# A conv-attention and mixture-of-experts layer on one core: where the expert gates' transfers are issued inside a step

## The chip, the core and the metric

The kernel runs on 1 core of one Trainium2 chip. The metric is the device time of one execution in microseconds (us), lower being better. Five engines with their own instruction streams work side by side: TensorE (PE in the profile; its weight loads are PEld), VectorE (DVE), ScalarE (ACT), GpSimd (POOL) and SyncE (SP). SP computes nothing here; it issues nearly all transfers between DRAM and the on-chip memory, one after the other, and waits at each until what the transfer depends on is done.

## The reference

The input `x` is 2 x 128 x 256 x 256 in float32. The layer does two things to it.

```python
x = x + attention(ln_over_channels(x))        # 8x8 windows, keys from 12x12, 4 heads of 32,
                                              # a fixed mask, relative positions, out projection
t = tokens(x)                                 # 131072 tokens of 128 channels
p = softmax(ln(t) @ router_w + router_b)      # 8 experts
g, e = top_2(p);  g = g / sum(g)
t = t + sum over the two: g * (ln(t) @ expert_w[e] + expert_b[e])
```

Of the mask only keys at every second row and column are left, so the image falls into four independent planes (row parity by column parity), and a window has 4 x 4 queries and 6 x 6 keys in a plane.

## The kernel before

**Strips, planes, steps.** The image is worked in 64 strips of 8 rows (32 for each of 2 images). Each strip has 4 planes, so there are 256 planes, and the main loop runs over `n`, one plane a step, with 7 more steps at the end to drain what follows. A step does attention for plane `n` (`scores`, `attend`, `out_project`), the projections for plane `n + 1` (`project`), the norms of one row pair (512 tokens) of a finished strip and of one row pair of a coming strip (`norms`), and, for older row pairs, the routing (`route`, `spread`) and the experts (class `Experts`). The order on each engine is written out by hand: all five engines run what the loop emits, in that order (`manual_schedule`).

**The experts.** All 8 experts are computed for all tokens: the input, less its mean and times expert e's gate, is multiplied with expert e's weights, and the 8 products are summed in PSUM (`product`, L714: 2 matmul instructions each, 16 a step). A gate is one number for each token. `spread` transposes the gates (`gT`, L651) and writes them to a small DRAM buffer `gd` (L659). From there `fetch(e)` reads one expert's 512 gates into a tile `gb` and copies them to all 128 partitions on the way (L689, 256 KB written); `fetch_means` does so for the means (`sb`, L694) and `fetch_rstd` for the scale of the coming row pair (`rb`, L665). Ahead of each gate's transfer stands a tiny write into the tile (L686 a ScalarE copy, L688 a VectorE memset). It paces the transfer: SP can't issue it before that engine has come to this place in its order.

**Three objects at a time.** `new` is the row pair whose gates are fetched in this step; a step later it is `nxt`, and its multiplications run: `means` (L699, `xs`: input plus `sb`), then `times(e)` (L705, `xe` = `xs` * `gb`) on VectorE for experts 0, 1, 2, 3, 4, 6 and on GpSimd for 5 and 7. Then it is `ex`: products 0 to 3 end that step and products 4, 6, 7, 5 stand in the middle of the next, followed by `end` (L720: the sum is added to the image, and the row pair is stored, L750).

**Gates before.** `gb` has 8 buffers, one a gate. Gates 0, 1, 2 are paced by memsets among VectorE's multiplications, 3 and 6 by memsets later in its order, 4 by a ScalarE copy after the norms. Gates 5 and 7 are fetched in the next step, through `nxt`: 5 behind ScalarE's exponential of the routing (L618), 7 behind its copy of the values (L358). SP's order in a step is:

```text
gd, gd, vrows (1 or 2), rb, sb, vwin, vwin, gate 0, 1, 2, xt (load), gate 3, out (store),
gate 4, gate 6 | next step: gate 5, gate 7
```

**Values.** `send_values` writes the value rows of plane `n + 1` to DRAM (`vrows`, L369); `take_values` reads them back as windows (`vwin`, L381), in two transfers of 240 KB, one for each half of the partitions. The first waits for the `vrows` writes to land.

**GpSimd.** Each step it runs `behind(6)` (L709, a one-element copy that waits for VectorE's `times(6)`), `times(5)`, `ln1` (L276, which needs `rb`), in every fourth step `halo` (L250), and `times(7)`.

**TensorE's code.** Its instructions are laid out in blocks of `BLOCK` = 256. At the start of each step of 6 or more, `addr_align` (L823) places the step so that `FIRST_LIMIT` = 95 instructions lie ahead of the first block boundary; the next boundaries come after 351 and 607. A weight load and a matmul are one instruction each. In a step 32 + 128 pairs (L474, L491), then `pu` 2, `pv` 8, `pk` 2 and `pq` 2 pairs come first, so the boundary after 351 falls just behind the first pair of the expert products (L714), and the one after 95 inside L491.

**DMA counters.** The built program gives the transfers eight completion counters in turn; an issue waits until the transfer eight before it has landed.

Of the kernel before, what the change touches and what calls it, by code (L numbers as in the profile page):

```python
# [11 lines left out]
F32 = mybir.dt.float32  # L12
# [5 lines left out]
P = 128  # L18
# [33 lines left out]
def kernel(  # L52
# [16 lines left out]
    nc = tc.nc  # L69
# [8 lines left out]
    NT = CH // P  # L78
# [7 lines left out]
    gates = ctx.enter_context(tc.tile_pool(name="gates", bufs=2))  # L86
# [18 lines left out]
    def load_x(i, k, paced=False):  # L105

        if i >= len(strips):
            return
        b, s = strips[i]
        if k == 0:  # L110
            xt[i] = xpool.tile([P, R, W], F32, tag="xt", name=f"xt{i}")
        r = s * R + 2 * k
        if paced:
            nc.scalar.copy(xt[i][:, 2 * k, 0:1], onesm[:, 0:1])
        nc.sync.dma_start(xt[i][:, 2 * k : 2 * k + 2, :], x[b, :, r : r + 2, :])
# [248 lines left out]
    def send_values(n, sent):  # L364

        i, pl = divmod(n, 4)
        for part, vr in sent:
            for k, at, m in runs(i, part):
                nc.sync.dma_start(  # L369
                    vrows[pl][1 : PC + 1, at : at + m, :],  # L370
                    vr[:, k - part[0] : k - part[0] + m],
                )

    def take_values(n):

        for half in range(2):
            src = vrows[n % 4][half * HP * 8 : half * HP * 8 + KC].rearrange("c r d -> (c r) d")
            src = src.unsqueeze(1)
            dims = [list(d) for d in src.ap]
            dims[1] = [8 * KR * P, HP]  # L380
            nc.sync.dma_start(  # L381
                vwin[n % 2][half * SLOT : half * SLOT + NK],
                bass.AP(src.tensor, src.offset, dims),
            )
# [77 lines left out]
    def scores(n, state):  # L462


        qs, kk, au = state["qs"], state["kk"], state["au"]
        turn = place(n // 4, 0) // 2
        att = ps_att.tile([P, 4, 512], F32, tag="att", name=f"att{n}")
        sc = att[:, :, 0:HQ]
        for w in range(2):
            for half in range(2):  # L470
                rows = slice(half * SLOT, (half + 1) * SLOT)
                for h in range(HEADS):
                    hp = slice(h * DH, (h + 1) * DH)
                    nc.tensor.matmul(  # L474
                        sc[rows, h].rearrange("p (t w z) -> p t w z", w=2, z=16)[:, :, w],
                        lhsT=keys[hp, turn, w],
                        rhs=au[hp, half * NP + w : (half + 1) * NP : 2].rearrange(
                            "p t a s -> p t (a s)"
                        ),
                        start=(w == 0),  # L480
                        stop=False,
                    )
        for t in range(HP):
            if t == HP // 2:
                yield
            for half in range(2):
                rows = slice(half * SLOT, (half + 1) * SLOT)
                m0 = 2 * (half * HP + t)
                for h in range(HEADS):
                    hp = slice(h * DH, (h + 1) * DH)  # L490
                    nc.tensor.matmul(  # L491
                        sc[rows, h, 32 * t : 32 * t + 32],
                        lhsT=kk[hp, half * HP + t, :],
                        rhs=qs[hp, m0 : m0 + 2].rearrange("p m a s -> p (m a s)"),
                        start=False,
                        stop=(t == HP - 1),
                    )
        pT = work.tile([P, HEADS, HQ], F32, tag="pT", name=f"pT{n}", bufs=1)
        nc.scalar.activation(pT, att[:, :, 0:HQ], AF.Exp)  # L499
        state.update(att=att, pT=pT)  # L500
        yield
# [166 lines left out]
    def to_all(gd, j):  # L668

        return gd[j * NT : (j + 1) * NT].rearrange("r k -> (r k)").partition_broadcast(P)  # L670

    class Experts:
# [7 lines left out]
        def fetch(self, e, eng):  # L680


            nm = "_".join(str(v) for v in (*self.at, e))
            self.gb[e] = gates.tile([P, NT * P], F32, tag="gb", name=f"gb{nm}", bufs=8)
            if eng is nc.scalar:
                eng.copy(self.gb[e][:, 0:1], onesm[:, 0:1])  # L686
            else:
                eng.memset(self.gb[e][:, 0:1], 0.0)  # L688
            nc.sync.dma_start(self.gb[e], to_all(self.gd, e))  # L689
# [55 lines left out]
    to_store = []  # L745

    def store(i, k):
        b, s = strips[i]
        r = s * R + 2 * k
        nc.sync.dma_start(out[b, :, r : r + 2, :], xt[i][:, 2 * k : 2 * k + 2, :])  # L750
        if k == R // 2 - 1:
            xt.pop(i)
# [4 lines left out]
    n_planes = 4 * len(strips)  # L757
# [45 lines left out]
    gated, ex, nxt = None, NoExperts(), NoExperts()  # L803
    last = ctile([P, 1], "last")
    pool, dve = nc.gpsimd, nc.vector

    ET = mybir.EngineType
    with tc.manual_schedule(engines={ET.PE, ET.DVE, ET.Activation, ET.Pool, ET.SP}):
        for n in range(n_planes + 7):
            i, pl = divmod(n, 4)  # L810
            score, attn, outp, ahead, norm, rout = none, none, none, none, none, none
            if n < n_planes:
                score = scores(n, states[n])
                attn = attend(n, states[n])
                outp = out_project(n, states[n])
            if n + 1 < n_planes:
                states[n + 1] = {}
                ahead = project(n + 1, states[n + 1])

            if 6 <= n < n_planes:
                nc.tensor.addr_align(BLOCK, offset=BLOCK - FIRST_LIMIT)  # L823


            next(score, None)
            new, row = NoExperts(), None
            if gated and gated[0]:
                rout = route(*gated[0], *gated[2])
            next(rout, None)  # L830
            nxt.fetch(5, nc.scalar)
            for _ in rout:
                pass
            next(score, None)
            next(ahead, None)
            nxt.fetch(7, nc.scalar)
            if gated:
                f, c, made = gated
                gd = spread(f, c, made[0], f"_{n}")
                new = Experts(*f, gd) if f else new  # L840
            if n + 1 < n_planes:
                send_values(n + 1, states[n + 1]["sent"])
            if gated and c:
                row = (*c, fetch_rstd(gd, f"_{n}"))
            next(ahead, None)
            if n + 1 < n_planes:
                states[n + 1]["shift"]()
            next(ahead, None)
            next(ahead, None)
            for e in (4, 6, 7, 5):  # L850
                ex.product(e)


            f = (i - 1, pl) if 0 < i <= len(strips) else None
            c = row_at(n)
            if f or c:
                norm = norms(f, c, f"_{n}")
            next(norm, None)
            next(attn, None)
            nxt.means()  # L860
            new.fetch_means()
            if n + 1 < n_planes:
                take_values(n + 1)
            for e in (0, 1, 2, 3):
                nxt.times(e, dve)
            new.fetch(0, dve)
            for e in (4, 6):
                nxt.times(e, dve)
            new.fetch(1, dve)
            ex.end()  # L870
            new.fetch(2, dve)
            next(attn, None)
            next(attn, None)


            ex = nxt
            next(norm, None)
            load_x((n + 9) // 4, (n + 9) % 4, paced=True)
            new.fetch(3, dve)
            while to_store:  # L880
                store(*to_store.pop())
            next(ahead, None)
            ex.product(0)
            made = next(norm, None)
            ex.product(1)
            ex.product(2)
            new.fetch(4, nc.scalar)
            nxt.behind(6)
            nxt.times(5, pool)
            if row:  # L890
                ln1(*row, pool)
            if pl == 3 and i + 2 < len(strips):
                halo(i + 2)
            nxt.times(7, pool)
            if n + 2 < n_planes:
                borders(n + 2)
            next(outp, None)
            ex.product(3)
            next(outp, None)
            new.fetch(6, dve)  # L900
            gated, nxt = (f, c, made) if made else None, new
            states.pop(n, None)

# [58 lines left out]
```

## Time and profile before

| | |
|---|---|
| time, median of 3 runs (lowest to highest) | 4413.72 us (4412.22 to 4419.66) |
| the profiled execution: its time, its span | 4415.92 us, 4414.1 us |
| granted TensorE clock, mean | 0.992 |
| PEld busy | 2453.1 us (56%) |
| VectorE busy | 3844.2 us (87%) |
| ScalarE, GpSimd busy | 1455.9 us (33%), 1092.5 us (25%) |
| HBM read and written | 863.78 and 143.75 MB, 228 GB/s over the span |

The page of the profile gives the busy time of each engine, the costliest groups of instructions (line, engine, operation, what is written and read, number, busy time and mean, and the idle time ahead of them with what ended it), the transfers by kind with the median time from issue to landing, and the DMA queues. The view of waits lists who waited for whom: total, number of times, longest. The timeline lists instructions in order of time: start in us, duration in us, engine, line, operation, tile, and in brackets the idle time ahead of it. "issue" there means that the profile shows nothing waited for. The view of windows gives each engine's busy time in a stretch and, last, the mean busy share of the DMA engines and the rate in GB/s.

### The profile page before, as it was taken

What the parts mean: (1) busy time and instruction counts of PE and PEld (TensorE: products, weight loads), DVE (VectorE), ACT (ScalarE), POOL (GpSimd) and SP (SyncE); (2) the same over time, 40 slices, a digit from 0 to 9 for tenths busy, and PEclk for the clock granted to TensorE, in tenths of its full rate; (3) what the DMA queues carried; (4) which work ended last, traced back from release to release, by engine and by line L of the source; (5) the groups of instructions that cost most, each with busy time, mean ns of one, the idle gap of its engine ahead of it and who ended that gap; (6) DMA issues with size and microseconds to landing.
All of it is one profiled execution on the core that took longest, in us unless ns stands there. A gap on an engine that the chain in (4) does not pass through costs nothing. (4 is left out here: it accounts for less than half of the span.)

```text
span 4414.1 us, 224656 instructions
## 1 busy us (share of the span) xinstructions
PE 4254.2 (96%) x94273; PEld 2453.1 (56%) x94273; DVE 3844.2 (87%) x11850; ACT 1455.9 (33%) x3774; POOL 1092.5 (25%) x1126
## 2 busy tenths in 40 slices
PE   7899999999999999999999999999999999999987
PEld 4555555555555555555555555555555555555553
DVE  5788889888898988898888889988888888888877
ACT  3333333333333333333333333333333333333321
POOL 1122222222222222222222222222222222222211
PEclk9999999999999999999999999999999999999998
DMA  4677777777787777777878777777778777777865
GB/s 121 201 246 229 244 232 241 246 234 233 233 242 232 242 238 235 244 234 243 243 233 243 231 242 232 243 239 239 242 229 244 238 236 233 232 232 239 243 195 183
DMA packets 824580, 1022.19 MB, mean 232 GB/s; under 512 B 137634, under 2 KB 409634, under 8 KB 823594
## 3 DMA queue, kind: packets, MB, share of 16 engines
q1 hardware_dynamic: 822864, 1007.52, 74.6%
q8 instruction: 769, 12.60, 1.2%
q14 instruction: 217, 1.78, 0.1%
q10 hardware_dynamic: 730, 0.29, 0.0%
HBM read 863.78 MB, written 143.75 MB: 228 GB/s over the span
## 5 line engine op out<-in xcount | busy, mean ns | idle before, releaser
L714 PE MATMUL acc<-xe,ew 128*128 128x512 f32 x4096 | 1935.8, 602 | 66.7 <-issue 44.9
L714 PEld LDWEIGHTS acc<-xe,ew 128*128 128x128 f32 x4096 | 759.2, 190 | 1001.6 <-issue 931.2
L705 DVE TENSOR_TENSOR xe<-xs,gb 128x512 f32<-128x512 f32 x1536 | 951.0, 687 | 12.3 <-DMA gb<-gd 2.2
L709 POOL COPY last<-xe 128x1 f32<-128x1 f32 x256 | 47.0, 184 | 3119.1 <-DVE gb L688 3109.9
L705 POOL TENSOR_TENSOR xe<-xs,gb 128x512 f32<-128x512 f32 x512 | 650.8, 1272 | 2.5 <-PE acc L714 1.6
L276 POOL TENSOR_TENSOR xn<-xt,rb 128x512 f32<-128x512 f32 x249 | 374.0, 1502 | 171.5 <-DMA rb<-gd 165.4
L491 PE MATMUL att<-qs,kcol 32*64 32x32 f32 x32768 | 396.9, 226 | 4.8 <-issue 4.7
L491 PEld LDWEIGHTS att<-qs,kcol 32*64 32x64 f32 x32768 | 394.4, 131 | 6.3 <-issue 5.8
L522 PEld LDWEIGHTS att<-pT,vwin 64*32 64x32 f32 x32768 | 348.0, 105 | 37.5 <-issue 0.4
L522 PE MATMUL att<-pT,vwin 64*32 64x32 f32 x32768 | 343.3, 200 | 0.2 <-issue 0.2
L350 PEld LDWEIGHTS pv<-wt,xn 128*128 128x128 f32 x2048 | 270.5, 192 | 127.4 <-issue 80.1
L434 ACT COPY kcol<-pk 128x560 f32<-128x560 f32 (+2 forms) x344 | 318.9, 927 | 52.4 <-PE pk L423 49.0
L499 ACT ACTIVATE pT<-att 128x1024 f32<-128x1024 f32 x256 | 261.9, 1023 | 221.3 <-PE att L491 220.7
L532 DVE STREAM_TRANSPOSE sT<-att 128x512 f32<-128x512 f32 x256 | 183.5, 717 | 133.4 <-PE att L522 124.1
L445 PE MATMUL pq<-xn,wt 128*128 128x512 f32 x512 | 272.8, 614 | 23.4 <-DVE uT L413 21.4
L408 PE MATMUL pu<-xn,wrel 128*128 128x512 f32 x512 | 293.0, 654 | 0.0
L574 ACT ACTIVATE sq<-xt 128x512 f32<-128x512 f32 x505 | 291.8, 629 | 0.0
L397 DVE STREAM_TRANSPOSE au<-auT 128x512 f32<-128x512 f32 x256 | 272.5, 1064 | 9.0
L550 PE MATMUL po<-o,wt 128*128 128x512 f32 x512 | 265.1, 599 | 8.2 <-DVE o L542 5.8
L350 PE MATMUL pv<-wt,xn 128*128 128x128 f32 x2048 | 271.3, 275 | 0.9 <-issue 0.9
L423 PE MATMUL pk<-xn,wt 128*128 128x512 f32 (+2 forms) x528 | 263.4, 581 | 2.4 <-issue 1.3
L474 PEld LDWEIGHTS att<-au,keys 32*64 32x64 f32 x8192 | 117.2, 132 | 227.7 <-PE po L550 183.5
(2696 smaller groups left out, 4884.0 us busy)
## 6 DMA issues: line engine op xcount, KB each, us to landing
gb<-gd SPq DMA_DIRECT2D x2048, 256.0 KB, 5.7
vwin<-vrows SPq DMA_DIRECT2D x512, 240.0 KB, 5.4
xt<-in_x_dram SPq DMA_DIRECT2D x256, 256.0 KB, 6.4
sb<-gd SPq DMA_DIRECT2D x256, 256.0 KB, 4.2
out_dram<-xt SPq DMA_DIRECT2D x256, 256.0 KB, 6.0
rb<-gd SPq DMA_DIRECT2D x249, 256.0 KB, 3.4
vrows<-vr SPq DMA_DIRECT2D x168, 256.0 KB, 4.0
vrows<-vr SPq DMA_DIRECT2D x160, 128.0 KB, 3.6
```

The costliest lines, as they stand in the source:

```text
L276: eng.tensor_tensor(xn[i % 2][:, :, :, k, 1 : PC + 1], ln1_src(i, k).rearrange("p (y j x) -> p y x j", y=2, x=2), rb.rearrange("p (y j x) ...
L350: nc.tensor.matmul(pv[:, j * P : (j + 1) * P], lhsT=xp[:, k, 1 : PC + 1], rhs=wv, start=True, stop=True,)
L397: nc.vector.transpose(au.rearrange("p m a s -> p a s m"), auT[n % 2])
L408: nc.tensor.matmul(pu, lhsT=wrel, rhs=inner, start=True, stop=True)
L434: nc.scalar.copy(places[:, 1 : NP - 1], windows(new[:, :, KC - 3 :], 0, NP - 2))
L445: nc.tensor.matmul(pq, lhsT=wq, rhs=inner, start=True, stop=True)
L491: nc.tensor.matmul(sc[rows, h, 32 * t : 32 * t + 32], lhsT=kk[hp, half * HP + t, :], rhs=qs[hp, m0 : m0 + 2].rearrange("p m a s -> p (m a ...
L522: nc.tensor.matmul(av[hp, half, 32 * t : 32 * t + 32], lhsT=vv[rows, t, hp], rhs=pT[rows, h, 32 * t : 32 * t + 32], start=True, stop=True,)
L550: nc.tensor.matmul(po, lhsT=wo, rhs=state["o"].rearrange("p f z -> p (f z)"), start=True, stop=True)
L574: nc.scalar.activation(sq, src, AF.Square)
L705: eng.tensor_tensor(self.xe[e], self.xs, self.gb.pop(e), ALU.mult)
L714: nc.tensor.matmul(self.acc, lhsT=ew[:, e, :], rhs=self.xe.pop(e), start=(e == 0), stop=not self.xe)
```

## The change

`gb` gets 10 buffers. All 8 gates of `new` are fetched in its own step, each paced by a VectorE memset; the two fetches through `nxt` in the next step and the ScalarE copies are gone. Gate 0 now stands behind `times(0)` and `times(1)`, ahead of the reads of the values; the two halves of these are issued apart. The load of `x` and the store move up, and the means' transfer (`sb`) moves to the end. SP's order becomes:

```text
gd, gd, vrows (1 or 2), rb, gate 0, vwin half 0, gate 1, xt (load), gate 2, gate 3, vwin half 1,
out (store), gate 4, gate 6, gate 5, gate 7, sb
```

The order of work on TensorE, and of all other work on VectorE, ScalarE and GpSimd, stays as it was. Each step has 8 memsets on VectorE in place of 5, and no gate copy on ScalarE in place of 3.

```diff
-    def take_values(n):
+    def take_values(n, halves=(0, 1)):
-        for half in range(2):
+        for half in halves:
...
-            self.gb[e] = gates.tile([P, NT * P], F32, tag="gb", name=f"gb{nm}", bufs=8)
+            self.gb[e] = gates.tile([P, NT * P], F32, tag="gb", name=f"gb{nm}", bufs=10)
...
             next(rout, None)
-            nxt.fetch(5, nc.scalar)
             for _ in rout:
                 pass
             next(score, None)
             next(ahead, None)
-            nxt.fetch(7, nc.scalar)
...
             nxt.means()
-            new.fetch_means()
-            if n + 1 < n_planes:
-                take_values(n + 1)
-            for e in (0, 1, 2, 3):
+            for e in (0, 1):
                 nxt.times(e, dve)
             new.fetch(0, dve)
+            if n + 1 < n_planes:
+                take_values(n + 1, (0,))
+            for e in (2, 3):
+                nxt.times(e, dve)
+            new.fetch(1, dve)
+            load_x((n + 9) // 4, (n + 9) % 4, paced=True)
             for e in (4, 6):
                 nxt.times(e, dve)
-            new.fetch(1, dve)
+            new.fetch(2, dve)
             ex.end()
-            new.fetch(2, dve)
+            new.fetch(3, dve)
+            if n + 1 < n_planes:
+                take_values(n + 1, (1,))
+            while to_store:
+                store(*to_store.pop())
             next(attn, None)
+            new.fetch(4, dve)
             next(attn, None)
+            new.fetch(6, dve)
+            new.fetch(5, dve)
...
             next(norm, None)
-            load_x((n + 9) // 4, (n + 9) % 4, paced=True)
-            new.fetch(3, dve)
-            while to_store:
-                store(*to_store.pop())
             next(ahead, None)
             ex.product(0)
             made = next(norm, None)
+            new.fetch(7, dve)
+            new.fetch_means()
             ex.product(1)
             ex.product(2)
-            new.fetch(4, nc.scalar)
...
             next(outp, None)
-            new.fetch(6, dve)
             gated, nxt = (f, c, made) if made else None, new
```

## The prediction

> **What bounds the kernel now.** First the page: who is busy, and at which lines.
>
> ```profile
> PE 4254.2 (96%) x94273; PEld 2453.1 (56%) x94273; DVE 3844.2 (87%) x11850; ACT 1455.9 (33%) x3774; POOL 1092.5 (25%) x1126
> ...
> q1 hardware_dynamic: 822864, 1007.52, 74.6%
> q8 instruction: 769, 12.60, 1.2%
> ...
> L714 PE MATMUL acc<-xe,ew 128*128 128x512 f32 x4096 | 1935.8, 602 | 66.7 <-issue 44.9
> ...
> gb<-gd SPq DMA_DIRECT2D x2048, 256.0 KB, 5.7
> ```
>
> TensorE bounds it, and it is late only here and there. I took the start of each step from the trace (the first L474 matmul) and looked at steps 8 to 246, 239 of them: they take 4015.6 us, 16.80 each. The shortest that recurs is 16.27 us, with no wait of TensorE in it; 47 steps are within 0.03 of it. So 0.53 us a step, some 127 us, is all that any change off TensorE can win. Measuring from line to line in each step, it splits into 0.28 just behind the first matmul of the expert products (in 101 steps), 0.21 between `pk` L423 and the end of `pq` L445, 0.03 inside L491, 0.01 elsewhere.
>
> The first of these, in the timeline (step from 2003.27):
>
> ```profile
> 2007.97 0.32 SPq L689 DMA_DIRECT2D gb<-gd  x1
> 2008.38 1.69 SPq L659 DMA_DIRECT2D gd<-gT  x2
> 2008.79 0.59 PE L714 MATMUL acc<-xe,ew 128*128 128x512 f32 x1
> 2008.98 0.66 DVE L699 TENSOR_TENSOR xs<-xt,sb 128x512 f32<-128x512 f32 x1
> 2010.12 1.05 SPq L369 DMA_DIRECT2D vrows<-vr  x2
> 2010.23 2.74 PE L714 MATMUL acc<-xe,ew 128*128 128x512 f32 x6 [0.85 <-issue]
> 2012.00 0.32 SPq L665 DMA_DIRECT2D rb<-gd  x1
> ```
>
> The matmul after the gap is the second half of a product that is already running, so no data are missing. The instruction queue moved 12.60 MB in 769 packets, 3 a step of 16 KB, and 12.60 MB over the 188,546 instructions of PE and PEld is 67 bytes each: it brings TensorE's code in blocks of about 256, and the boundary after 351 lies here. The block's packet starts 3.80 us after the step's start at the median (10% to 90%: 2.98 to 4.61); where it starts later than about 3.8 the products stop. What delays it is seen in the windows of that step (last columns: DMA share, GB/s):
>
> ```profile
> 2003.27:2007.27 4.00, 4.00 (x172) 3.47 (x172) 3.57 (x18) 1.33 (x4) 0.00 (x0) 1.00 0.95 311
> 2007.27:2011.27 4.00, 3.15 (x8) 1.31 (x7) 3.90 (x8) 3.72 (x9) 0.00 (x0) 1.00 0.71 215
> 2011.27:2013.27 2.00, 2.00 (x5) 0.58 (x4) 2.00 (x5) 0.34 (x2) 0.00 (x0) 1.00 0.50 143
> 2013.27:2016.27 3.00, 3.00 (x178) 2.56 (x178) 1.80 (x6) 0.00 (x0) 2.14 (x3) 1.00 0.82 209
> 2016.27:2020.55 4.28, 4.28 (x10) 1.61 (x9) 3.49 (x15) 0.50 (x3) 2.00 (x2) 1.00 1.06 252
> ```
>
> The DMA engines are full from +13 us of a step to +4 of the next, and half idle from +8 to +10. The second loss is VectorE's: `pq` waits for `uT` (L413). VectorE's own round is 16.0 us, only 0.27 under TensorE's, and it is stretched where GpSimd runs late, at line L235:
>
> ```profile
> 189.25 1.50 POOL L276 TENSOR_TENSOR xn<-xt,rb 128x512 f32<-128x512 f32 x1 [1.26 <-DMA rb<-gd]
> ...
> 190.71 1.27 POOL L705 TENSOR_TENSOR xe<-xs,gb 128x512 f32<-128x512 f32 x1
> 190.75 1.25 DVE L235 SCALAR_TENSOR_TENSOR u__9_3099<-u__9_3099,epsc 128x8 f32<-128x8 f32 x1
> ```
>
> L235 takes 0.17 us alone; here it ends with GpSimd's multiplication. The waits say why GpSimd is late, and what holds SP:
>
> ```profile
> POOL xn L276 <- DMA rb<-gd: 165.4, 129, 29.2
> ...
> SPq L689 <- ACT gb L686: 870.7, 518, 16.9
> SPq L665 <- DMA gd<-gT: 327.3, 241, 2.7
> SPq L381 <- DMA vrows<-vr: 198.5, 229, 2.3
> ```
>
> **Part 1: gate 7 out of SP's way (gain).** `gT` is ready at +3.9, but `gd` goes at +5.1, behind gate 7 (2007.97 above), which waits for ScalarE's copy. In the changed order `gd`, `vrows` and `rb` go 1.2 us earlier; `rb`, landed at +12.0 now, lands near +10.8, ahead of GpSimd's need at about +11.8. I took each step's GpSimd chain and shortened its wait for `rb` by 1.2: the time that VectorE loses at L235 and L238 falls from 0.26 to 0.10 us a step (what is left is mostly the `halo` copy of every fourth step). In proportion, the 0.21 at `pq` falls by **0.13**. Between nothing (TensorE hides it by another stop) and 0.21.
>
> **Part 2: memsets (loss, small).** 3 more on VectorE, 3 x 0.059 (L688) = 0.18 us. Behind a long instruction they cost nothing: from `xe` 3 to `xe` 4, with a memset between, 0.610 us; from `xe` 0 to `xe` 1, without, 0.609. Only the second of a pair in a row (gates 6 and 5) can show, 0.06. I take **0.02**; range 0 to 0.18. VectorE's next work behind each is on its path to `pq`. ScalarE loses 3 copies of 0.18, which nothing waits for. The buffers' waits are for multiplications long done: gate 0 takes the tile of gate 5 of two steps back, which GpSimd read half a step before.
>
> **Part 3: `sb` last (loss).** `xs` (L699) stands at the head of all multiplications and needs `sb`. Now `sb` lands at +13.3, half a step early. Afterwards it is the last of a train. In the saturated stretch now, 9 transfers land from +16.75 (second `vwin`) to +23.43 (gate 5 of the next step): 0.74 each. The two `vwin` with what is around them take 3.4 (`sb` +13.3 to +16.75), or 2 x 1.1 by their own spacing. The train behind `rb`: 8 gates, `xt`, `out`, `sb` = 11 x 0.74 = 8.2, plus 2.2 to 3.4, from +10.8: **`sb` lands at +21.2 to +22.4**, in a floor step's terms +4.9 to +6.1 of the next. `xs` is ready at +5.7 (2008.98 - 2003.27). The mean margin is +0.2 us, and landings scatter by about 0.75 (gate 6 now lands from +4.92 to +7.14, 10% to 90%). A margin of 0.2 with such a scatter loses 0.2 us on average; as a step made longer by it gives the next train more room, I charge half: **0.10**. Range 0 (margin 0.8) to 0.4 (margin -0.4). Queued behind `xs`: six `xe`, `end`, `sT`, on GpSimd `times(5)`, and the memsets that start the next train.
>
> **Part 4: the code blocks (loss).** Now the block at 351 gets through about 0.9 us before gate 4 lands (+4.74), while gates 6 and 5 are issued later (+0.3 and +1.2) and gate 7 after it. In the new order all are issued by about +0.3. If it gets through ahead of `sb`, but behind gate 7 (landing 0.74 before `sb`, middle +4.8), it starts at +3.9, as now; if behind `sb`, at +4.6, a stop of 0.8 in each step. One in ten for that: **0.08**. The idle stretch from +8 to +10 is filled, which helps, but gate 7 comes into the train (0.74), so the train doesn't end much earlier. The block for L491 (packet now at +13.15 median; 17 steps stop) is asked for near +11.4, where now two `vwin` lie ahead and then four or five transfers: about 1 us later, and the share of steps over the limit goes from 7% to some 20%: **0.06**. For both together: from -0.28 (all gone) to +0.5.
>
> [...]
>
> **Sum.** -0.13 + 0.02 + 0.10 + 0.08 + 0.06 = +0.13 us a step, x 239 = +31 us on the profiled execution's 4415.92: 4447. Its first 8 steps and the drain (157.6 and 240.9 us) I leave as they are: there gates, not their order, are waited for, a few us either way. The median of the runs lies 2.2 us lower: **4445 us**.
>
> **Rivals.**
> (a) *Faster: the train ends early.* `vwin` apart cost 1.1 each, `sb` has its 0.8 us of margin, and the block passes ahead of gate 7. For it: the idle quarter of DMA time between +4 and +13. Against: the work in the train grows by a gate. Parts 1 and 2 alone give -0.11 x 239 = -26 us; with half of the 0.28 gone as well, -60: 4355 to 4390, 4370 in the middle.
> (b) *Much slower: `sb` late in nearly every step.* Price: at 3.4 us for the `vwin` plus the window of eight transfers in flight, landing at +6.4 or later; from margin -0.7 on each step pays 0.35 for `sb` and 0.3 at the blocks: less part 1, 0.5 x 239: 4510 to 4560.
> (c) *No difference*: stops at the code block or `sb` eat part 1 exactly, 4405 to 4423. It includes that the change doesn't do what it says: SP, held by `vwin` or by the eight in flight, pushes gates into the next step as before.
>
> **How the numbers follow.** Forecast (slower by 0.2% to 1.6%) 0.44, (a) 0.35, (b) 0.11, (c) 0.10. What a measurement here can tell from no change is about 0.2%. Faster 0.35, same 0.10, slower 0.55. The range leaves out the lower third of (a) and most of (b): 4362 to 4525. The forecast's own: 4423 to 4485.
>
> **What would show it.** Right: `rb` landing 1.2 us earlier and L276's wait for it nearly gone, L235 at 0.17 in most steps; a new wait of L699 for `sb` of tens of us; "issue" ahead of L714 no smaller than 66.7 us; more idle time ahead of L491 than 4.8. Wrong: L699 never waits for `sb`, L714's stops shrink, and the DMA share falls well below 0.9 before +3.

## The result, and the profile after

The changed kernel takes 4564.82 us (median of 4 runs, 4554.95 to 4573.21) beside 4413.48 us (4 runs, 4412.22 to 4419.66): ratio 1.0339, interval 1.0314 to 1.0364. It is slower by 151 us, and outside the predicted range. The profiled execution took 4554.95 us, with a span of 4553.2 us: 139 us over that of before. Counted from first L474 to first L474, steps 8 to 246 take 17.31 us each in place of 16.80, which is 123 us of it; the drain takes 257.1 us in place of 240.9, the first 8 steps 157.8 in place of 157.6.

On the page after, the chain that ended last is the first thing to read. Before, hardly any of it had a share, since it ended in the drain. Now it goes back through the whole run:

```profile
PE 4301.7 (94%) x94273; PEld 2453.3 (54%) x94273; DVE 3872.6 (85%) x12618; ACT 1391.8 (31%) x3006; POOL 1083.5 (24%) x1126
...
DMA 35%; PE 30%; DVE 22%; issue 11%; ACT 1%; SPq 0%; DVEq 0%; POOL 0%; POOLq 0%; ACTq 0%
DMA sb<-gd 17%; DMA gb<-gd 17%; PE acc L714 13%; DVE xe L705 7%; PE att L522 3%; PE pq L445 2%; PE att L491 2%; DVE xs L699 2%; PE pu L408 2%; PE pv L350 1%; PE pk L423 1%; PE att L512 1%; PE po L550 1%; DVE sT L532 1%; PE plt L580 1%
...
L714 PE MATMUL acc<-xe,ew 128*128 128x512 f32 x4096 | 1941.1, 601 | 94.3 <-issue 45.9
...
L491 PE MATMUL att<-qs,kcol 32*64 32x32 f32 x32768 | 403.8, 226 | 13.7 <-issue 13.4
...
gb<-gd SPq DMA_DIRECT2D x2048, 256.0 KB, 6.4
...
sb<-gd SPq DMA_DIRECT2D x256, 256.0 KB, 5.9
```

`sb` and the gates in flight make up 34% of it, and `xs` (L699) and `xe` (L705) stand between them: `sb` lands, `xs` runs, the multiplications follow, the memsets behind them release the next gates, and behind those stands the next `sb`. That is a closed loop, and TensorE is in it with 30% only. In the groups L714 has lost 27.6 us more than before, but its "issue" part is as it was (44.9, now 45.9); L491 has gone from 4.8 to 13.7 us.

The waits of the changed kernel (who waits for whom, total, times, longest), all engines and then SP's alone:

```profile
PEld pq L445 <- DVE uT L413: 215.9, 231, 1.8
DVE xs L699 <- DMA sb<-gd: 210.2, 206, 9.5
...
POOL xn L276 <- DMA rb<-gd: 76.4, 5, 29.3
```

```profile
SPq L689 <- DVE gb L688: 723.8, 1117, 2.8
...
SPq L665 <- DMA gd<-gT: 171.4, 199, 2.1
SPq L694 <- DMA gb<-gd: 134.6, 195, 2.0
```

The line of `pq` in the kernel before:

```profile
PEld pq L445 <- DVE uT L413: 162.9, 235, 2.2
```

VectorE waits for `sb` in 206 steps, 0.80 us a step over steps 8 to 246; before, it did so once. GpSimd's wait for `rb` is gone but for 5 places (129 before), and yet `pq` waits longer, 215.9 us in place of 162.9, in nearly as many places. On SP the gates wait for VectorE's memsets, 1117 times, up to 2.8 us: where VectorE is late, the train is late too. SP's last line (L694) is new: in 195 steps the issue of `sb` itself waits until a gate has landed, by the eight completion counters in turn (of the 1674 issues for which the trace has the landing of the transfer eight before, none comes ahead of it, the closest 0.016 us behind).

One step in the timeline (from 1798.92 to 1815.88):

```profile
1799.20 0.42 SPq L694 DMA_DIRECT2D sb<-gd  x1
...
1805.81 0.69 DVE L699 TENSOR_TENSOR xs<-xt,sb 128x512 f32<-128x512 f32 x1 [0.58 <-DMA sb<-gd]
...
1805.96 0.32 SPq L665 DMA_DIRECT2D rb<-gd  x1
...
1806.54 1.91 DVE L705 TENSOR_TENSOR xe<-xs,gb 128x512 f32<-128x512 f32 x3
...
1807.93 0.32 SPq L689 DMA_DIRECT2D gb<-gd  x1
...
1813.78 1.27 POOL L705 TENSOR_TENSOR xe<-xs,gb 128x512 f32<-128x512 f32 x1
...
1814.15 0.92 DVE L235 SCALAR_TENSOR_TENSOR u__103_33041<-u__103_33041,epsc 128x8 f32<-128x8 f32 x1
```

and the windows of that step (DMA share and GB/s last):

```profile
1802.92:1806.92 4.00, 3.73 (x9) 1.30 (x8) 3.30 (x7) 3.63 (x8) 0.00 (x0) 1.00 0.52 166
1806.92:1808.92 2.00, 2.00 (x17) 0.70 (x22) 2.00 (x5) 0.32 (x2) 0.00 (x0) 1.00 0.46 133
```

`xs` starts 6.9 us into the step; gate 0, the head of the train, goes at +9.0, since it stands behind two multiplications that stand behind `xs`. Until then the DMA engines are half idle, as they were before (0.50 from +8 to +10): the stretch that the change was to use stays empty. And a late `xs` makes `xe` 6 late, which GpSimd waits for (L709), so its last multiplication still lies on L235 (0.92 us here, 0.17 alone), although `rb` is in time.

### The profile page after: what moved, and what is told of

It reads as the page before. It is cut to its first block, busy times and chain, and to the rows that moved or that the text cites. A ratio compares the mean times of both kernels' runs of the same rounds, so it can differ in the third digit from the quotient of the medians.

```text
span 4553.2 us, 224436 instructions
## 1 busy us (share of the span) xinstructions
PE 4301.7 (94%) x94273; PEld 2453.3 (54%) x94273; DVE 3872.6 (85%) x12618; ACT 1391.8 (31%) x3006; POOL 1083.5 (24%) x1126
## 4 chain that ended last, share of the span: by engine, by line
DMA 35%; PE 30%; DVE 22%; issue 11%; ACT 1%; SPq 0%; DVEq 0%; POOL 0%; POOLq 0%; ACTq 0%
DMA sb<-gd 17%; DMA gb<-gd 17%; PE acc L714 13%; DVE xe L705 7%; PE att L522 3%; PE pq L445 2%; PE att L491 2%; DVE xs L699 2%; PE pu L408 2%; PE pv L350 1%; PE pk L423 1%; PE att L512 1%; PE po L550 1%; DVE sT L532 1%; PE plt L580 1%
## 5 line engine op out<-in xcount | busy, mean ns | idle before, releaser
L714 PE MATMUL acc<-xe,ew 128*128 128x512 f32 x4096 | 1941.1, 601 | 94.3 <-issue 45.9
L714 PEld LDWEIGHTS acc<-xe,ew 128*128 128x128 f32 x4096 | 759.1, 190 | 1040.3 <-issue 952.4
L705 DVE TENSOR_TENSOR xe<-xs,gb 128x512 f32<-128x512 f32 x1536 | 952.6, 686 | 9.0
L709 POOL COPY last<-xe 128x1 f32<-128x1 f32 x256 | 47.0, 183 | 3364.5 <-DVE gb L688 3352.5
L705 POOL TENSOR_TENSOR xe<-xs,gb 128x512 f32<-128x512 f32 x512 | 649.8, 1270 | 0.9 <-PE att L522 0.2
L491 PE MATMUL att<-qs,kcol 32*64 32x32 f32 x32768 | 403.8, 226 | 13.7 <-issue 13.4
L491 PEld LDWEIGHTS att<-qs,kcol 32*64 32x64 f32 x32768 | 399.5, 131 | 17.0 <-issue 16.1
L276 POOL TENSOR_TENSOR xn<-xt,rb 128x512 f32<-128x512 f32 x249 | 374.0, 1502 | 76.6 <-DMA rb<-gd 76.4
L522 PEld LDWEIGHTS att<-pT,vwin 64*32 64x32 f32 x32768 | 348.1, 105 | 44.5 <-issue 7.5
L699 DVE TENSOR_TENSOR xs<-xt,sb 128x512 f32<-128x512 f32 x256 | 176.4, 689 | 211.0 <-DMA sb<-gd 210.2
L522 PE MATMUL att<-pT,vwin 64*32 64x32 f32 x32768 | 344.4, 200 | 6.2 <-issue 6.2
L550 PE MATMUL po<-o,wt 128*128 128x512 f32 x512 | 263.6, 596 | 8.4 <-DVE o L542 5.8
L474 PEld LDWEIGHTS att<-au,keys 32*64 32x64 f32 x8192 | 121.7, 132 | 259.6 <-issue 131.9
```

Source lines behind the costliest of these rows:

```text
L276: eng.tensor_tensor(xn[i % 2][:, :, :, k, 1 : PC + 1], ln1_src(i, k).rearrange("p (y j x) -> p y x j", y=2, x=2), rb.rearrange("p (y j x) ...
L491: nc.tensor.matmul(sc[rows, h, 32 * t : 32 * t + 32], lhsT=kk[hp, half * HP + t, :], rhs=qs[hp, m0 : m0 + 2].rearrange("p m a s -> p (m a ...
L522: nc.tensor.matmul(av[hp, half, 32 * t : 32 * t + 32], lhsT=vv[rows, t, hp], rhs=pT[rows, h, 32 * t : 32 * t + 32], start=True, stop=True,)
L550: nc.tensor.matmul(po, lhsT=wo, rhs=state["o"].rearrange("p f z -> p (f z)"), start=True, stop=True)
L705: eng.tensor_tensor(self.xe[e], self.xs, self.gb.pop(e), ALU.mult)
L714: nc.tensor.matmul(self.acc, lhsT=ew[:, e, :], rhs=self.xe.pop(e), start=(e == 0), stop=not self.xe)
```

## The experiments

The excess of each step over 16.27 us, cut at the same lines as in the prediction, is the measure for all kernels. All in us a step, steps 8 to 246 of the profiled run; "products" is the stop behind the first matmul of the products, "L491" includes what it costs in `pu` and `pv` behind it, "pq" is from `pk` to the end of `pq`, "xs" is VectorE's wait for `sb`, "rb" GpSimd's wait for `rb`, the last column the median start of the code packets for the products and for L491's block, counted from the start of one step (L491's block is used in the next).

| kernel | median us | ratio (interval) | products | L491 | pq | rest | xs | rb | packets at |
|---|---|---|---|---|---|---|---|---|---|
| before | 4413.48 | | .28 | .04 | .21 | 0 | 0 | .39 | 3.80, 13.16 |
| changed | 4564.82 | 1.0339 (1.0314–1.0364) | .29 | .09 | .40 | .27 | .80 | 0 | 4.11, 14.68 |
| e1 | 4644.92 | 1.0540 (1.0519–1.0560) | .25 | .92 | .04 | .17 | 0 | .01 | 3.97, 16.16 |
| e2 | 4519.39 | 1.0263 (1.0246–1.0280) | .32 | .44 | .03 | .14 | 0 | .01 | 3.96, 15.27 |
| e3 | 4475.49 | 1.0166 (1.0144–1.0188) | .08 | .07 | .47 | .09 | .31 | .39 | 3.25, 13.48 |
| e5 | 4451.15 | 1.0115 (1.0080–1.0150) | .08 | .45 | .05 | .08 | 0 | 0 | 3.56, 15.24 |
| e6 | 4415.5 | one run | .10 | .21 | .07 | .11 | .05 | 0 | 3.22, 14.25 |
| e7 | 4414.68 | 1.0018 (1.0003–1.0033) | .28 | .05 | .21 | .01 | 0 | .37 | 3.72, 13.13 |
| e8 | 4423.21 | 1.0032 (1.0021–1.0043) | .01 | .06 | .45 | 0 | 0 | .71 | 2.97, 13.96 |
| e9 | 4380.6 | 0.9938 (0.9917–0.9959) | .07 | .02 | .26 | 0 | 0 | .37 | 3.36, 12.87 |
| e10 | 4354.42 | 0.9878 (0.9862–0.9894) | .14 | .04 | .06 | .01 | 0 | .04 | 3.25, 12.85 |
| e11 | 4393.82 | 0.9958 (0.9943–0.9973) | .34 | .04 | .05 | 0 | 0 | .04 | 3.84, 12.93 |
| e12 | 4349.08 | 0.9858 (0.9839–0.9877) | .08 | .06 | .10 | .01 | 0 | .14 | 3.12, 13.54 |
| e13 | 4457.15 | 1.0098 (1.0076–1.0120) | .52 | .04 | .08 | 0 | 0 | .19 | 4.17, 13.47 |

The kernel before, beside them, had a median of 4407.5 us (e1 to e5), 4408.39 (e6 to e9), 4410.88 (e10 to e12) and 4414.73 (e13).

Two theories matter. Theory 1: the time comes from `sb` at the end of the train, by the loop above; with `sb` early it goes. Theory 3: what counts is where the train of gates lies beside the two code packets of TensorE; a train that starts earlier lies ahead of the request for L491's block, one that starts later ahead of the products' block. The traces don't show the requests themselves: the places that the expectations name (+0.9, +5.9 and +11.4) are my estimates from where TensorE comes to each boundary (in before the 15th matmul of L491, the first of the products and the 105th of L522 end at +0.83, +6.17 and +11.10 at the median). Over all kernels the three packets of a step start at +1.4, +4.9 and +11.2 at the earliest, the second and the third ahead of the places named. The other views that an expectation names are told in it.

**e1: the changed kernel with `sb` early.**

```diff
             nxt.means()
+            new.fetch_means()
...
             new.fetch(7, dve)
-            new.fetch_means()
```

> The changed kernel with the means' transfer (sb) put back to its old place, right behind the means addition and so ahead of gate 0; everything else of the change stays. Theory 1 (sb as the last of the train makes xs at L699 wait, 0.80 us a step in the changed kernel, and all else follows from it): L699 no longer waits (under 10 us in all, against 210 us), and the time falls to 4390 to 4450 us. Theory 2 (the denser train itself costs the time, by late code blocks for TensorE and late gates, and L699's wait is only where it shows): the time stays above 4500 us, with more 'issue' time ahead of L714, or waits of the multiplications for gates in place of the one for sb.

It came out 80 us slower than the changed kernel, where theory 1 had it at 4390 to 4450 us. `xs` no longer waits and `pq` is free (.04), but L491 now stops in 164 places:

```profile
L491 PE MATMUL att<-qs,kcol 32*64 32x32 f32 x32768 | 431.7, 227 | 147.5 <-issue 147.3
```

Theory 1 alone fell. With `xs` in time the train starts earlier: its first gate is issued 8.2 us into the step at the median, 9.3 in the changed kernel and 11.5 before. And the packet for L491's block starts at 16.16, 14.68 and 13.16.

**e2: the changed kernel without the wait.** `xs` takes the means of the row pair before, so the wait goes while the order of the transfers stays.

```diff
-            nc.vector.tensor_add(self.xs, self.src, self.sb)
+            nc.vector.tensor_add(self.xs, self.src, kept[max(0, len(kept) - 2)])
```

> The changed kernel in its own order, sb last, but the addition at L699 reads the means that were fetched one step earlier (two buffers for sb), so it computes with the means of another row pair. The transfers and their order are those of the changed kernel; only the wait for the last of the train is gone. Theory 1: L699 doesn't wait, time 4390 to 4450 us, and within 20 us of the run with sb early. Theory 2: above 4500 us, since the train is as dense as before.

Some 40 to 45 us are won of 151, and the place of the loss changes as in e1: `pq` .03, L491 .44. So the wait for `sb` costs time, and also holds back a train that would cost nearly as much at L491.

**e3: before, with only `sb` moved to the end** (`new.fetch_means()` behind `new.fetch(6, dve)`).

> The kernel before with one edit: the means' transfer is issued last in its step, behind gate 6 (gates 5 and 7 still follow in the next step). Theory 1: sb lands about 5.5 us after an issue near +0.7, that is at +6.0 to +6.5 of the next step, against a need at +5.7, so L699 waits 0.3 to 0.8 us a step and the time rises to 4460 to 4540 us. Theory 2: no gate is moved, the train is no denser, so the time stays at 4405 to 4425 us.

This is part 3 by itself: 68 us by the medians. In the profiled run it is 0.17 us a step, some 40 us, and 15 us more in the drain.

```profile
DVE xs L699 <- DMA sb<-gd: 93.0, 120, 8.5
```

`xs` waits in 120 steps and VectorE comes late to `pq` (.47); the stop at the products shrinks to .08, its packet being earlier (3.25).

**e5: before, with only gate 7 out of the way of `gd`.**

```diff
-            nxt.fetch(7, nc.scalar)
             if gated:
...
                 row = (*c, fetch_rstd(gd, f"_{n}"))
+            nxt.fetch(7, nc.scalar)
```

> The kernel before with one edit: gate 7's fetch, still in the next step and behind ScalarE's copy, is issued behind the transfer of rb and no longer ahead of gd, vrows and rb. It tests part 1 of the prediction alone. If part 1 holds: rb lands about 1 us earlier, GpSimd's wait for it (165 us in all) falls under 60 us, VectorE's L235 takes 0.17 us in more steps, and the time falls by 0.13 us a step, to 4370 to 4395 us. If GpSimd's lateness isn't what holds pq: 4405 to 4420 us.

Part 1 by itself does what it says for `rb`, and loses 44 us, which neither expectation had:

```profile
POOL xn L276 <- DMA rb<-gd: 77.3, 7, 29.1
PE att L491 <- issue: 68.8, 114, 2.4
```

`rb` is in time, `pq` falls from .21 to .05 and the products' stop to .08; L491 pays .41 for both. Its packet now starts at 15.24, 2.08 us later than before: gate 7 and what follows `rb` in SP's order go out before +11.2, the earliest start of this packet in any kernel (gates 0, 1 and 2 at +10.0, +10.6 and +11.1 at the median; gate 0 went at +11.5), and so lie ahead of it.

**e6: the changed kernel without gates 5 and 7** (experts 5 and 7 take the gates of 4 and 6), so the train is two transfers shorter.

> The changed kernel, but gates 5 and 7 are not transferred (nor paced); GpSimd multiplies with gates 4 and 6 in their place, so experts 5 and 7 get wrong gates. The order is the changed one, sb last; the train is 2 x 256 KB shorter, about 1.5 us of 12. Theory 3 (TensorE's code blocks and sb both queue behind the train, so its length and not its order makes the loss): sb lands about 1.5 us earlier, L699 waits under 0.2 us a step in place of 0.80, the stops behind the first product, in L491 and in L522 shrink too, and the time falls below the kernel before, to 4310 to 4400 us. Theory 4 (the order or the memsets on VectorE cost by themselves): it stays above 4480 us.

`xs` waits in 22 places (21.5 us) and the one run took about the time of before; the 4310 to 4400 expected was missed. So the length of the train decides over `sb`; with it short, L491 keeps .21.

**e7: before, with three more memsets on VectorE**, at the places where the change adds them.

> The kernel before with three more one-column memsets a step on VectorE, onto a scratch tile, at the places where the change puts gates 4, 5 and 7; no transfer moves. Part 2 of the prediction: 0.02 us a step, 5 us in all, 4405 to 4425 us. Theory 4: 0.06 us for each, 0.18 a step, so 4440 us or more.

0.02 to 0.03 us a step: part 2 was right.

**e8: before, with gates 4 and 6 fetched in the next step, beside gate 5.**

```diff
-            nxt.fetch(5, nc.scalar)
+            for e in (4, 6, 5):
+                nxt.fetch(e, nc.scalar)
```

> The kernel before with the opposite edit: gates 4 and 6 too are fetched in the next step, with gate 5, behind ScalarE's exponential of the routing (L618), which is just behind the place where TensorE asks for the code block that it needs in the products. Theory 3: that block then finds two transfers fewer ahead of it, its packet starts 1 to 1.5 us earlier (median near 2.5 in place of 3.8), the stops behind the first product (0.28 us a step) nearly go, and the time falls to 4345 to 4400 us, or stays if the freed time goes into pq or L491 as it did where only gate 7 was moved. If the code block isn't delayed by data issued ahead of it: no earlier packet.

The stop at the products is gone (.01): its packet goes out first, at 2.97. But `rb` comes later still (.71) and `pq` takes it all back (.45).

**e9: three bundles.** Gates 4, 6, 5, 7 go in the next step at the place of gate 5, the load of `x` right behind `sb`; gate 0, both `vwin` and gates 1, 2, 3 behind `end`, that is about where the estimate above has the request for L491's block.

> A version built on theory 3: the kernel before with the transfers in three bundles, each issued behind one of TensorE's three requests for code (about +0.9, +5.9 and +11.4 us of a step), so that the DMA engines have drained when the next request comes. Gates 4, 6, 5, 7 go behind L618 of the next step; gd, vrows, rb, sb and the load of x behind the second request; gate 0, both vwin, gates 1, 2, 3 and the store from behind L720 on. Theory 3: all three blocks start within 3 us of their request, TensorE's stops fall from 0.53 to under 0.25 us a step, 4290 to 4360 us, faster than both kernels. If code isn't held up by the train ahead of it: 4400 us or more, since the work is the same.

Both packets are early (3.36, 12.87) and 28 us are won, short of the 4290 to 4360 us expected: the stops fell to .35 and not under .25, and `pq` is what is left.

```profile
PEld pq L445 <- DVE uT L413: 182.6, 238, 2.5
POOL xn L276 <- DMA rb<-gd: 162.0, 118, 29.7
```

**e11, e10, e12: GpSimd does `ln1` last.** Its order becomes `times(5)`, `times(7)`, `ln1`, `halo`, so a late `rb` holds back only `ln1`; alone (e11), with e9 (e10) and with e8 (e12).

```diff
             nxt.times(5, pool)
+            nxt.times(7, pool)
             if row:
                 ln1(*row, pool)
...
-            nxt.times(7, pool)
```

> The kernel before with GpSimd's order alone changed: times(5), times(7), ln1, halo. It tests part 1 without moving a transfer: there the gain was 0.13 us a step at pq. If VectorE is held only by GpSimd's wait for rb: L235's excess falls from 0.26 to 0.10 us a step and the time to 4375 to 4395 us. If, as with gate 7 moved, the earlier VectorE makes the train earlier against the code block for L491: pq's loss goes, L491's stop grows, 4400 to 4450 us.

> The version with three bundles, and GpSimd's order changed: times(5), times(7), then ln1 and halo, so that the wait for rb stands behind both multiplications (in the version with three bundles GpSimd still waits 0.37 us a step for rb, and pq loses 0.26). Theory 3 with part 1's mechanism (VectorE's L235 held by a late GpSimd): GpSimd's wait for rb goes under 0.05 us a step, L235's excess from 0.34 to about 0.10, pq's loss to about 0.1, and the time from 4381 to 4335 to 4365 us. Rival (VectorE with less slack only meets the next wait): 4370 to 4385 us.

> The kernel with gates 4 and 6 in the next step, and GpSimd's order changed as in the other two runs. With gates 4 and 6 moved, the stop behind the first product had gone (0.28 to 0.01 us a step) but GpSimd's wait for rb had doubled (0.71) and pq lost 0.45. With ln1 last that wait goes: pq's loss under 0.15, the rest as it was, 4320 to 4365 us. Rival: the stops move to L491 instead, 4390 us or more.

Alone it frees `pq` (.05) without touching a transfer, and 0.06 of that goes to the products' stop: 17 us. With e9's order (e10) `pq` falls to .06 and the products' stop doubles to .14. With e8's order, which had bought the products' packet with a late `rb`, both are had: 4349.08 us, 1.4% below the kernel before and, with e10 (the intervals overlap), the fastest. TensorE is at 97%:

```profile
PE 4235.2 (97%) x94273; PEld 2455.4 (56%) x94273; DVE 3812.1 (88%) x11594; ACT 1483.9 (34%) x4030; POOL 1092.4 (25%) x1126
```

**e13: all gates in their own step, but late.** As the changed kernel, with `sb` and the load early and all gates behind `end`.

> The changed kernel with its main idea kept (all 8 gates fetched within their own step, paced by VectorE, 10 buffers) but the train started later: sb and the load of x right behind rb, and gate 0, both vwin, gates 1, 2, 3, the store and gates 4, 6, 5, 7 from behind L720 on. No transfer waits at the end for VectorE's addition, and little is in flight when TensorE asks for the block for L491 (near +11.4). Theory 3: L491's block is as early as before (median near 13, stop under 0.06 us a step) and L699 doesn't wait, but ten transfers and two vwin now lie ahead of the request near +0.9, so the block for the products starts near +5 and stops TensorE by 0.6 to 1.2 us a step: 4420 to 4560 us. Rival (L491's block and the wait for sb were all that the change cost; where the train ends doesn't matter): 4330 to 4390 us, with the stop behind the first product at or under 0.28 us a step.

The mirror of e1: L491 is as before (.04), and the products stop by .52, their packet starting at 4.17 (.6 to 1.2, and +5, were expected).

```profile
L714 PE MATMUL acc<-xe,ew 128*128 128x512 f32 x4096 | 1947.0, 601 | 113.9 <-issue 94.5 <-DVE gb L688 17.0 <-DVE xt L720 0.8
```

Eight gates in one bundle, with values, load or store among them, lie ahead of the one packet or the other: e1 and e13 are the two ends, and e9 and e12, which cut it in pieces between the requests as estimated, lose least.

## Why the prediction was wrong

**The reading held.** In before and in e7 to e13 the three places named there hold the whole excess but for 0.01. The limit at the packet is sharp. TensorE stops for code in three places, always the same: behind the first matmul of the products, the 15th of L491 and the 105th of L522, where the boundaries after 351, 95 and 607 lie. The next matmul comes a nearly fixed time after the end of the block's packet: in before, changed kernel, e1, e2 and e5 the medians at each place are 1.36 to 1.45 us, and 10% to 90% of the stops lie from 1.25 to 1.58.

**Part 1** (-0.13): the mechanism is right (e5: `pq` from .21 to .05; L276's wait from 129 to 5 places in the changed kernel, `rb` landing at +10.68 where 10.8 was said). As a gain it failed twice: by itself it starts the train into L491's packet (e5, +.41), and in the changed kernel GpSimd is late by `xe` 6 in place of `rb`, so that `pq` rose by .19 (with `xs` in time, in e2, it is .03).

**Part 2** (+0.02): right (e7).

**Part 3** (+0.10) is the step that failed, in its size. `sb` was to land at +21.2 to +22.4, that is +4.9 to +6.1 of the next step. It landed at +24.45, +7.1 of the next (medians of the 100 steps for which the trace has its landing). The term that was mis-sized is the train, 11 x 0.74 plus 2.2 to 3.4, so 10.4 to 11.6 us from `rb`'s landing; it took 13.8. The price was right for the back of the train and wrong for its front: gate 3, the sixth transfer behind `rb`, lands 8.5 us after it, where the sum has 4.8 to 5.4, and the seven behind gate 3 take 5.3 us, where it has 5.5 to 6.1. The sum let the train run without a break from `rb` on. But each gate is released by a memset in VectorE's order: SP waits 724 us for memsets, and the windows above show 0.46 where I wrote that the idle stretch is filled.

How much of it is lateness handed on through `xs`, e2 tells: there `xs` waits for nothing, and `sb` still lands at +23.37, 1.0 to 2.2 later than forecast and behind the need. SP waits for memsets there too (in e2 the lines lie two lower):

```profile
SPq L691 <- DVE gb L690: 588.0, 906, 2.5
```

So `sb` comes late by the order of the train alone, and the loop adds 1.1 us. I had seen that a longer step gives the next train more room, and charged half for it; with the wait in place `sb` lands later in its step, not earlier. SP also issues `sb` at +1.1 of the next step at the median, not at +0.3 (+0.1 in e2). What makes the rest of the slow front in e2 was not taken apart. Alone, on the order of before, part 3 costs 0.17 a step (e3). In the changed kernel the 0.80 of L699 show as .19 at `pq` and .27 in "rest": 0.09 ahead of product 0, which waits for `end` (L720) on the same late VectorE, 0.15 ahead of L474 and 0.03 in L522 (below). The drain, left as it was give or take a few us, grew by 16.

**Part 4** (+0.08 products, +0.06 L491): L491 rose by .05, about as said; the products by .01. That L491 came out as said is luck: it is small only because the late `xs` holds back the train. Take the wait away (e1, e2) and L491 costs .92 and .44. So the two losses stand in for each other, part 4 was too small for the train that part 3 had in mind, and no version with all gates in their own step came out faster.

**The rivals.** What happened is (b), `sb` late in nearly every step, priced at 4510 to 4560 (the time is just above it) and given 0.11. Its price is met in part by luck: it had 0.3 us a step at the code blocks, which took .06, and 0.35 for `sb`, which cost more. (a) counted on slack in which the train ends early; e1 and e13, where `sb` is out of the way, are both slower than the kernel before. Of what would show it, L276's wait, the idle time at L714 (94.3 us) and L491 came as for right (the 66.7 us, called "issue" there, are all of the idle time ahead of L714; "issue" was 44.9 of them and is 45.9 now); L235 at 0.17 did not (VectorE's excess at L235 and L238 is .29, it was .26), and L699's wait was 210 us, not tens.

**The rest, and what is open.** Ahead of each step `addr_align` (L823) puts instructions that do nothing, 31 in a step by the trace. They stand in TensorE's order behind `po` (L550), which waits for VectorE's `o` (L542). In before and in the changed kernel they start 0.16 us after `o` ends and take 2.27 us. Before, the last is through 0.38 us ahead of L474, so they cost nothing; in the 105 steps of the changed kernel where L474 comes late, it ends 0.06 us ahead of it. A late `o` thus delays the next step by the padding: 0.15 us a step in the changed kernel, 0.07 in e3. In e1, e2, e5 and e6 "rest" is the stop in L522, at the boundary after 607 (0.18, 0.15, 0.08 and 0.12 us a step). In e1 the block's packet starts at +9.8 at the median where TensorE stops, and at +7.7 where it doesn't:

```profile
PE att L522 <- issue: 33.3, 63, 1.5
```

Open is how data hold up a packet of code: whether it stands behind the transfers issued before it, or only shares the DMA engines with them while they are full. In before the products' packet starts later where the last gate issued up to +1.7 us lands later (correlation 0.85 in the 122 steps for which the trace has that landing), which fits both; all the runs that move a train change both.

## What to carry to other kernels

When a transfer moves to the end of a train, follow it through what it releases to the head of the next train: if that head is paced by work that needs this transfer, lateness circulates, and an average margin of 0.2 us says nothing. Price a train at the rate of a full stretch only where nothing releases its transfers one by one. Here transfers of data delayed transfers of code (in e5, with gate 0 issued at +10.0 in place of +11.5, the packet of L491's block started at 15.24 in place of 13.16): estimate from the trace when each code block is asked for, and put trains right behind a request, in pieces, rather than ahead of one (e9, e12). And before moving transfers to bring data earlier, see whether the engine that waits can do something else first; moving one GpSimd multiplication ahead of `ln1` gave `pq` as much (e11, .05) as moving gate 7 (e5, .05), and cost 0.06 at the products where that cost 0.41 at L491.

## What the runs showed of the hardware

In e1 some stops of TensorE cost more than their length, through the granted clock. TensorE's timeline in a step with a stop of 2.23 us in L491:

```profile
741.64 1.36 PE L491 MATMUL att<-qs,kcol 32*64 32x32 f32 x113 [2.23 <-issue]
742.93 2.07 PE L408 MATMUL pu<-xn,wrel 128*128 128x512 f32 x2
744.80 1.78 PE L350 MATMUL pv<-wt,xn 128*128 128x128 f32 x8
746.42 1.02 PE L423 MATMUL pk<-xn,wt 128*128 128x512 f32 x2
```

and the windows before, in and after it (the granted clock is the third number from the end):

```profile
739.50:742.90 3.40, 1.26 (x113) 1.25 (x112) 2.54 (x10) 0.10 (x1) 0.00 (x0) 1.00 1.09 297
742.90:746.30 3.40, 3.40 (x18) 2.34 (x11) 1.19 (x4) 1.02 (x1) 0.00 (x0) 0.50 0.59 201
746.30:749.70 3.40, 3.40 (x10) 1.63 (x10) 3.37 (x7) 2.78 (x5) 0.00 (x0) 1.00 0.43 126
```

`pu` takes 2.07 us (1.13 in a step at full clock, that from 465.12) and `pv` 1.78 (1.05): the clock was 0.50 for one window of 3.41 us and full again behind it. In e1, 15 of the 18 stops of 1.85 us or more had such a window behind them, 6 of 11 from 1.5 to 1.85, and 7 of 44 from 1.0 to 1.5; the mean clock fell from 0.992 to 0.980. What e1 loses in `pu` and `pv` in all is .15 of its .92 at L491.
